# Graph attention on one core: a third tile picked in every fifth step, the edge bias written by ScalarE, picking from step 0 to 96, and one tile of sixteen steps fetched row by row from ScalarE's queue

## The chip, the core and the metric

The kernel runs on one core of a Trainium2 chip. The metric is the time of one execution on the device in microseconds (us). The kernel before takes 1790.06 us (median of three runs, 1789.95 to 1790.13). A profile is a trace of one further execution.

## The reference

One layer of graph attention with a residual and a layer norm. There are N = 6250 nodes with 64 features and E = 206250 edges, sorted by destination; four heads of 16.

```python
Qh = (x @ Wq.T + bq).reshape(n, H, D)
Kh = (x @ Wk.T + bk).reshape(n, H, D)
Vh = (x @ Wv.T + bv).reshape(n, H, D)
Ee = (edge_attr @ We.T + be).reshape(-1, H, D)
score = (Kh[src] * Qh[dst] * (1.0 / np.sqrt(D)) * Ee).sum(-1)
score = jnp.exp(jnp.clip(score, -5.0, 5.0))
msg = Vh[src] * score[..., None]
wV = jax.ops.segment_sum(msg, dst, num_segments=n)
x = _layernorm(x + wV.reshape(n, H * D))
```

## The kernel before

Edges are cut into 1612 tiles of 128, eight tiles to a group (202 groups). The main loop has 105 steps: 97 of two groups (16 tiles) and then 8 of one group.

A prologue computes a table of keys and values for every node (`kv_tab`, in DRAM) and a table of queries (`q3_tab`). The keys and values of the first four groups are computed directly from gathered rows of x (`xs`): a transpose, a copy by ScalarE and matmuls with `wkv`, half a group at a time.

In a step, the rows of `kv_tab` of each tile's 128 source nodes have to come into one of five buffers `kvs`. They get there in four ways:

- One indirect DMA for each tile, issued by POOL (`gather_kv`, L402). In step s the gathers of step s + 4 are issued; a buffer is free once the message of the step that used it is made.
- Two tiles of a step are **picked** by TensorE, two steps ahead of use, in steps 4 to 94. ScalarE writes the source numbers less 50 times the column (`sources`, L466), TensorE turns them into `from_b` (`sources_turned`, L471), VectorE compares them with block numbers (`hots`, L481, in two halves) and TensorE multiplies the one-hot matrix with the table of x in three bf16 parts (`picks`, L491, 25 matmuls a half). The three parts are added (`picked`, L498), turned (`picked_turned`), and multiplied with the weights (`picked_kv`, L513 to L516), whose result ScalarE copies to `kvs`.
- Every sixth step one tile is fetched row by row by 128 plain DMAs from SP's queue, spread over the six steps before (`fetch_rows`, L540 and L544; the row numbers are loaded to registers).
- The first four groups, as said.

The table of parts is made in the loop's first steps: SP loads pieces of x, ScalarE and VectorE split them (`table_parts`).

The rest of a step: `spread` (L555) and ScalarE's Square and Relu (`onehot_rows`, L572, and `onehot_rows_rest`, L577) make the one-hot rows of the next step's destinations; `queries` (L595) multiplies them with a window of queries; `edges` (L388 the bias, L391 the values) makes edge values in PSUM; `products` (L602, L603), `scores` (L609 to L612, with ScalarE's Exp), `message` (L619, L622) and `minus` (L630, L632) give the message in three bf16 parts; `sums` (L638) multiplies it with one-hot edges (L585), and `add` (L652) adds the result to an accumulator. When a block of 128 nodes is complete it is closed (L668 to L678), and later normalised and stored.

The order of all instructions on each engine is that in which the code emits them: the schedule is written by hand. Each engine works through its own list in that order, and waits where data or a buffer is not ready. In PSUM, `small` is one tile that holds the turned sources, the scores and the sums; `pb` is a single buffer used by `spread` and by `picked_turned` and `picked_kv`.

Of the kernel before, what the change touches and what calls it, by code (L numbers as in the profile page):

```python
# [40 lines left out]
TB = 8  # L41
M0 = 4
# [21 lines left out]
LAST = NS - 8 - 3  # L64


def picks_in(s):
    return M0 <= s <= LAST

# [5 lines left out]
COLUMN = 2 * G - 3  # L75
# [27 lines left out]
def tile_gnn(ctx: ExitStack, tc: tile.TileContext, x, xT, wT, bias, beT, weT, eT, src, dst, dst_rows,  # L103
# [52 lines left out]
    bkv_p = consts.tile([3, G // 2, 2 * C], BF16, name="bkv_p")  # L156
    minus_b = consts.tile([P, P], BF16, name="minus_b")
# [26 lines left out]
    with tc.tile_pool(name="nodes", bufs=1) as nodes, \  # L184
# [36 lines left out]
        nc.sync.dma_start(be_sb, beT.to_broadcast([3, C]))  # L221
        nc.vector.memset(we_sb, 0.0)
# [147 lines left out]
        for g in range(XG):  # L370
            for h in range(2):
                tp = npsum.tile([P, 2, P], F32, name="tp", bufs=2)
                for u in range(2):
                    j = 4 * h + 2 * u
                    nc.tensor.transpose(tp[:, u, :],
                                        XS[g][:, j:j + 2, :].rearrange("p j c -> p (j c)"), ident)
                xe = nodes.tile([P, 2, P], F32, name="xe", bufs=2)
                nc.scalar.activation(xe, tp, AF.Copy)
                pv = npsum.tile([P, 4, 2 * C], F32, name="pv", bufs=2)
                nc.tensor.matmul(pv, ones_b, bkv_p, start=True, stop=False, skip_group_check=True)  # L380
                for u in range(2):
                    nc.tensor.matmul(pv[:, 2 * u:2 * u + 2, :], xe[:, u, :], wkv, start=False,
                                     stop=u == 1, skip_group_check=True)
                nc.scalar.activation(kv_of(g)[:, 4 * h:4 * h + 4, :], pv, AF.Copy)

    def edge_values(pe, et, n):

        nc.tensor.matmul(pe[:, :n, :], ones_b, be_p[:, :n, :], start=True, stop=False,  # L388
                         skip_group_check=True)
        for u in range(n // 2):  # L390
            nc.tensor.matmul(pe[:, 2 * u:2 * u + 2, :], et[:, u, :], we_sb, start=False,  # L391
                             stop=u == n // 2 - 1, skip_group_check=True)
# [13 lines left out]
    for g in range(XG, 2 * KVB - 2):  # L406
        for j in range(G):
            gather_kv(g, j)
# [3 lines left out]
    with tc.If(rv == 0) as branch:  # L412

        with tc.tile_pool(name="work", bufs=2) as work, \
# [5 lines left out]
            col, from0, from1 = (small[:, i * C:(i + 1) * C].bitcast(BF16) for i in range(3))  # L420
            from_b = from0, from1
            score_all = small[:, 3 * C:3 * C + 2 * G * H]
            pa = small[:, 4 * C:7 * C].rearrange("p (i c) -> p i c", i=3)
            nc.tensor.transpose(col, row_b[:, 0:1].to_broadcast([P, P]), ident_b)

            parts = accp.tile([P, NB, 3, C], BF16, name="parts")
            nc.vector.memset(parts, 0.0)
            NX = N // NB
            x_v = x.rearrange("(p b) c -> p b c", p=NX)
            n_picks = LAST - M0 + 1  # L430
            src_f = accp.tile([P, n_picks, 2], F32, name="src_f")
            t0 = (M0 + 3) * 2 * G - 2
            for i in range(2):
                nc.vector.tensor_copy(src_f[:, :, i],
                                      src_i[:, t0 + i:t0 + i + 2 * G * (n_picks - 1) + 1:2 * G])
            pick = fixed.tile([P, 4 * P], F32, name="pick")
            rows3 = pick[:, :6 * C].rearrange("p (k i c) -> p k i c", k=2, i=3)
            HOT, FAR, X = {}, {}, {}
# [5 lines left out]
            def table_parts(b):  # L444

                n = min(TB, NB - b)
                raw = work.tile([P, TB, C], F32, name="raw", bufs=1)
                nc.sync.dma_start(raw[:NX, :n], x_v[:, b:b + n, :])
                rest = pick[:NX, :n * C].rearrange("p (b c) -> p b c", b=n)
                nc.scalar.activation(rest, raw[:NX, :n], AF.Copy)  # L450
                nc.scalar.activation(parts[:NX, b:b + n, 0], raw[:NX, :n], AF.Copy)
                return rest

            def table_parts_rest(b, rest):
                n = min(TB, NB - b)
                nc.vector.tensor_sub(rest, rest, parts[:NX, b:b + n, 0])
                nc.scalar.activation(parts[:NX, b:b + n, 1], rest, AF.Copy)
                nc.vector.tensor_sub(parts[:NX, b:b + n, 2], rest, parts[:NX, b:b + n, 1])

            def sources(s, i):  # L460

                if picks_in(s):
                    FAR[s, i] = work.tile([P, P], BF16, name="far")
                    nc.scalar.activation(FAR[s, i], row50, AF.Identity,  # L466
                                         bias=src_f[:, s - M0, i:i + 1], scale=-1.0)

            def sources_turned(s, i):
                if picks_in(s):  # L470
                    nc.tensor.transpose(from_b[i], FAR.pop((s, i)), ident_b)  # L471
# [4 lines left out]
            def hots(s, i, h):  # L476

                if picks_in(s):
                    HOT[s, i, h] = work.tile([P, NB // 2, P], BF16, name="hot", bufs=4)
# [6 lines left out]
            def picks(s, i, h):  # L486
                if picks_in(s):
                    hot = HOT.pop((s, i, h))
                    for k in range(NB // 2):
                        b = h * NB // 2 + k  # L490
                        nc.tensor.matmul(rows3[:, i], hot[:, k, :], parts[:, b], start=b == 0,  # L491
                                         stop=b == NB - 1)

            def picked(s):

                if picks_in(s):
                    xp = work.tile([P, 2, C], F32, name="xp")
                    nc.vector.tensor_reduce(xp, rows3.rearrange("p k i c -> p k c i"), axis=AX.X,  # L498
                                            op=OP.add)
                    X[s] = xp  # L500

            def picked_turned(s):
                if picks_in(s):
                    room = psum.tile([P, G, P], F32, name="pb")
                    nc.tensor.transpose(room[:, 0, :], X[s].rearrange("p k c -> p (k c)"), ident)
                    xe = work.tile([P, P], F32, name="xe")
                    nc.scalar.activation(xe, room[:, 0, :], AF.Copy)
                    X[s] = xe, room[:, 4:6, :]

            def picked_kv(s):  # L510
                if picks_in(s):
                    xe, kv = X.pop(s)
                    nc.tensor.matmul(kv, ones_b, bkv_p[:, :2], start=True, stop=False,  # L513
                                     skip_group_check=True)
                    nc.tensor.matmul(kv, xe, wkv, start=False, stop=True, skip_group_check=True)  # L515
                    nc.scalar.activation(kvs[(s + 2) % KVB][:, 2 * G - 2:, :], kv, AF.Copy)  # L516

            def gather(s):
                for g in groups_of(s):
                    for j in range(tiles_of(g)):  # L520
                        if is_rowed(s) and (g - STEPS[s][0]) * G + j == COLUMN:
                            continue
                        if not picks_in(s - 2) or g == STEPS[s][0] or j < G - 2:
# [21 lines left out]

            def rows_fetched(s):
                if is_rowed(s):
                    nc.scalar.activation(kvs[s % KVB][:, COLUMN, :], RK.pop(s), AF.Copy)

# [10 lines left out]
            def edges(s, k):  # L560

                g = STEPS[s][0] + k
                if k == 0:
                    PE[s] = psum.tile([P, 2 * G, C], F32, name="pe")
                edge_values(PE[s][:, k * G:(k + 1) * G], ET[g], tiles_of(g))
# [134 lines left out]
            closed, scaled, normed = 0, 0, 0  # L700
            keys(0)
# [5 lines left out]
            onehot_edges(0)  # L707
            for s in range(NS):
# [9 lines left out]
                if more:  # L718
                    onehot_rows(nexts[0], spread(nexts[0]))
                    onehot_rows_rest(nexts[0])  # L720
# [4 lines left out]
                if nexts[1:]:  # L725
                    onehot_rows(nexts[1], spread(nexts[1]))
                making = [b for b in range(s * 2 * TB, (s + 1) * 2 * TB, TB) if b < NB]
                if making:
                    rest = table_parts(making[0])
                prod = products(s)  # L730
                picked(s - 1)
                if more:
                    edges(s + 1, 0)
                picks(s, 0, 0)
                score = scores(s, prod)
                if nexts[1:]:
                    onehot_rows_rest(nexts[1])
# [5 lines left out]
                picked_turned(s - 1)  # L743
                if nexts[1:]:
                    edges(s + 1, 1)
                minus(s, msg, 0)
                hots(s, 1, 0)
                picks(s, 0, 1)
                minus(s, msg, 1)
                picked_kv(s - 1)  # L750
# [5 lines left out]
                picks(s, 1, 0)  # L756
                sources(s + 1, 1)
                sources(s + 2, 0)
                if s + 1 < NS:
                    rows_fetched(s + 1)  # L760
                if more:
# [5 lines left out]
                hots(s + 1, 0, 0)  # L767
                hots(s + 1, 0, 1)
# [14 lines left out]
                for i, b in enumerate(making):  # L783
                    if i:
                        rest = table_parts(b)
                    table_parts_rest(b, rest)
# [4 lines left out]
            scales(B - 2, B - 1)  # L791
            norm(B - 2)
# [170 lines left out]
```

## Time and profile before

| what | value |
|---|---|
| median of three runs | 1790.06 us |
| profiled execution | 1789.88 us |
| its span, first to last instruction | 1788.0 us |
| matmul busy | 1638.5 us, 15751 instructions |
| VectorE busy | 1481.6 us |
| ScalarE busy | 914.0 us |
| POOL busy | 1337.4 us |
| mean granted TensorE clock | 0.951 |

The span is what the trace covers; the execution's own time is 1.9 us longer. PE is TensorE's matmuls, PEld its weight loads, DVE VectorE, ACT ScalarE, POOL GpSimd, SP SyncE; a q after the name is an engine's own queue of DMA and semaphore instructions. A line of the groups gives source line, engine, operation, what is written from what, shapes and count, then busy time, mean length in ns, and the idle time ahead of it with what ended it. A line of the timeline gives start and length in us. In a line of the waits stand the total, the number and the longest.

### The profile page before, as it was taken

How to read it: one execution, taken by the hardware profiler on the slowest of the kernel's cores; microseconds unless marked ns; L12 is line 12 of the kernel's file. 1: busy time of each engine (PE TensorE's matmuls, PEld its weight loads, DVE VectorE, ACT ScalarE, POOL GpSimd, SP SyncE). 2: the span in 40 equal slices, each digit the busy share in tenths (PEclk: the TensorE clock that was granted, in tenths of full speed). 3: DMA queues.
4: the chain of work that ended last, by engine and by line, in shares of the span. 5: the costliest groups of instructions: out<-in, count | busy, mean ns of one | idle time of the engine just before them, and what ended most of it. 6: DMA issues, size and time to landing. Idle time of an engine off the chain costs nothing.

```text
span 1788.0 us, 44286 instructions
## 1 busy us (share of the span) xinstructions
PE 1638.5 (92%) x15751; PEld 1369.6 (77%) x15751; DVE 1481.6 (83%) x1695; ACT 914.0 (51%) x1328; POOL 1337.4 (75%) x1427
## 2 busy tenths in 40 slices
PE   8978999999999998999999899999989998999864
PEld 8647888888888787787887778777877887787632
DVE  6459999999998898888889888888988888898654
ACT  3465555555554464454455445455544554455443
POOL 7777777777777777777777777777777777777774
PEclk9968999999999999999999999999999999999855
DMA  7443333333333333332333333323332333333331
GB/s 221 132 121 84 90 93 94 93 94 92 93 81 94 93 86 89 92 94 80 93 93 81 93 81 93 92 81 99 87 93 80 94 93 81 93 90 81 91 80 44
DMA packets 109970, 166.71 MB, mean 93 GB/s; under 512 B 69196, under 2 KB 71452, under 8 KB 109626
## 3 DMA queue, kind: packets, MB, share of 16 engines
q0 software_dynamic: 45280, 91.78, 19.4%
q1 hardware_dynamic: 64074, 71.01, 14.1%
q8 instruction: 125, 2.05, 0.5%
q10 hardware_dynamic: 384, 1.00, 0.3%
q14 instruction: 107, 0.88, 0.2%
HBM read 156.33 MB, written 7.33 MB: 92 GB/s over the span
## 4 chain that ended last, share of the span: by engine, by line
PE 38%; POOL 29%; issue 14%; DVE 13%; DMA 4%; ACT 3%; DVEq 0%; SPq 0%; POOLq 0%; ACTq 0%
POOL kv L402 29%; PE pick L491 18%; PE pe L391 5%; DVE hot L481 5%; DMA kv<-kv_tab,src_i 3%; PE pq L630 2%; PE small L638 2%; DVE prod L603 2%; DVE prod L602 2%; PE pb L555 2%; PE pe L388 2%; PE pb L515 1%; PE pq L595 1%; DVE pq L619 1%; PE ps L350 1%
## 5 line engine op out<-in xcount | busy, mean ns | idle before, releaser
L402 POOL DMA_INDIRECT kv<-kv_tab,src_i x1383 | 1305.3, 944 | 421.7 <-issue 399.8
L491 PE MATMUL pick<-parts,hot 128*128 128x192 bf16 x9100 | 828.3, 249 | 0.0
L491 PEld LDWEIGHTS <-hot 128*128 128x128 bf16 x9100 | 771.7, 99 | 38.1
L481 DVE TENSOR_TENSOR hot<-small,block 128x3200 bf16<-128x3200 bf16 x364 | 645.3, 1813 | 0.4 <-PE pick L491 0.4
L572 ACT ACTIVATE to<-pb,minus_row 126x1024 bf16<-126x1024 f32 x202 | 222.7, 1102 | 371.0 <-PE pb L555 367.2
L632 ACT ACTIVATE msg<-pq 128x1024 bf16<-128x1024 f32 (+2 forms) x210 | 207.6, 989 | 222.3 <-PE pq L630 222.3
L391 PEld LDWEIGHTS pe<-we_sb,et 128*128 128x128 f32 x1612 | 209.7, 203 | 133.4 <-issue 95.3
L602 DVE TENSOR_TENSOR prod<-kv,pq 128x1024 f32<-128x1024 f32 (+2 forms) x105 | 123.5, 1176 | 169.3 <-DMA kv<-kv_tab,src_i 52.0
L391 PE MATMUL pe<-we_sb,et 128*128 128x128 f32 x1612 | 250.3, 302 | 0.0
L577 ACT ACTIVATE to<-to,one_p 126x1024 bf16<-126x1024 bf16 x202 | 230.6, 1142 | 3.5
L638 PEld LDWEIGHTS <-of 128*128 128x128 bf16 x1612 | 145.3, 102 | 31.1 <-issue 7.9
L638 PE MATMUL small<-msg,of 128*128 128x192 bf16 x1612 | 161.9, 257 | 0.5 <-ACT msg L632 0.5
L388 PE MATMUL pe<-be_p,ones_b 3*128 3x512 bf16 x202 | 79.7, 395 | 86.3 <-DVE prod L603 86.1
L630 PE MATMUL pq<-msg,minus_b 128*128 128x512 bf16 x404 | 128.0, 396 | 33.1 <-ACT msg L622 19.5
L622 ACT ACTIVATE msg<-pq 128x1024 bf16<-128x1024 f32 (+2 forms) x105 | 103.8, 989 | 96.8 <-DVE pq L619 96.8
L609 DVE TENSOR_REDUCE small<-prod 128x64 f32<-128x1024 f32 (+2 forms) x105 | 123.6, 1177 | 14.5 <-PE small L471 8.8
L555 PE MATMUL pb<-key_rows,ident_b 112*128 112x512 bf16 x403 | 127.9, 400 | 2.8 <-ACT to L572 2.8
L603 DVE TENSOR_TENSOR prod<-prod,pe 128x1024 f32<-128x1024 f32 (+2 forms) x105 | 123.6, 1177 | 3.6
L619 DVE TENSOR_TENSOR pq<-kv,small 128x1024 f32<-128x1024 f32 (+2 forms) x105 | 123.4, 1175 | 1.4 <-ACT small L612 1.4
L585 DVE TENSOR_TENSOR of<-small,key 128x2048 bf16<-128x2048 bf16 (+2 forms) x105 | 122.9, 1171 | 0.3
L595 PEld LDWEIGHTS <-to 126*128 126x128 bf16 x1612 | 63.5, 101 | 25.3 <-issue 25.1
L612 ACT ACTIVATE small<-small 128x64 f32<-128x64 f32 (+2 forms) x105 | 21.7, 207 | 111.1 <-DVE small L611 109.2
(129 smaller groups left out, 996.4 us busy)
## 6 DMA issues: line engine op xcount, KB each, us to landing
et<-in_eT SPq DMA_DIRECT2D x100, 512.0 KB
rk<-kv_tab SPq DMA_DIRECT2D x1920, 0.5 KB
kv<-kv_tab,src_i POOLq DMA_INDIRECT x1383
qw<-q_tab SPq DMA_DIRECT2D x202, 15.8 KB
kv_tab<-kv_sb SPq DMA_DIRECT2D x5, 640.0 KB
q_tab<-q SPq DMA_DIRECT2D x5, 480.0 KB
acc<-in_x SPq DMA_DIRECT2D x48, 32.0 KB
out<-y SPq DMA_DIRECT2D x48, 32.0 KB
```

Source lines behind the costliest of these rows:

```text
L391: nc.tensor.matmul(pe[:, 2 * u:2 * u + 2, :], et[:, u, :], we_sb, start=False, stop=u == n // 2 - 1, skip_group_check=True)
L402: nc.gpsimd.indirect_dma_start(out=kv_of(g)[:, j, :], out_offset=None, in_=kv_tab[:, :], in_offset=bass.IndirectOffsetOnAxis(ap=src_i[:, t ...
L481: nc.vector.tensor_tensor(HOT[s, i, h].rearrange("p b (a c) -> p b a c", c=2), pairs(from_b[i])[:, None].to_broadcast(shape), block2[:, bl ...
L491: nc.tensor.matmul(rows3[:, i], hot[:, k, :], parts[:, b], start=b == 0, stop=b == NB - 1)
L555: nc.tensor.matmul(pb[:, b:b + 4, :], ident_b[:NR2, g // 2:g // 2 + 1].to_broadcast([NR2, P]), key_rows[:, g % 2, b * P:(b + 4) * P], star ...
L572: nc.scalar.activation(TO[g][:, :n, :], pb[:3 * W, :n, :], AF.Square, bias=minus_row3[:3 * W])
L577: nc.scalar.activation(TO[g][:, :n, :], TO[g][:, :n, :], AF.Relu, bias=one_p[:3 * W], scale=-1.0)
L602: nc.vector.tensor_mul(prod[:, :n, :], kvs[s % KVB][:, :n, :C], PQ[s][:, :n, :])
L603: nc.vector.tensor_mul(prod[:, :n, :], prod[:, :n, :], PE[s][:, :n, :])
L630: nc.tensor.matmul(msg[:, lo:hi, :], minus_b, M3[s][:, lo:hi, i, :], start=False, stop=True, skip_group_check=True)
L632: nc.scalar.activation(M3[s][:, :n, i + 1, :], msg[:, :n, :], AF.Copy)
L638: nc.tensor.matmul(PA[s], OH[s][:, j, :], M3[s][:, j], start=j == 0, stop=j == n - 1)
```

## The change

Five edits, in one diff:

- **A third tile.** In every fifth step (0, 5 ... 90) a third tile is picked, with its own hots, picks into a `pb` tile (`R3`), reduction (`picked_third`), a 64-column turn and a share in `picked_kv`.
- **Picking from step 0 to 96.** The table of parts is no longer made in the loop but in the prologue, from `xT_sb` by 50 transposes, interleaved with the first groups' keys and values, whose next half is turned one half ahead. The first hots stand ahead of step 0.
- **ScalarE's bias.** The bias matmul of `edges` is gone except for step 0; ScalarE writes the bias to PSUM (`biases`) and the edge matmuls add to it. The tile is now a fixed one, `pe_all`.
- **Rows from ScalarE's queue.** One tile in each of the steps 20, 36, 52, 68 and 84 is fetched by 128 row DMAs from ScalarE's queue, eight in each of the sixteen steps before (`fetch_rows2`).
- **The order of a step.** `spread` of the first next group comes after `sources_turned` and not first; `edges` of both groups come after the message; `picked_turned` and `picked_kv` come later. At the end `scales` and `norm` of one block move behind `roots` of the last.

```diff
+LAST = NS - 8 - 1
+def is_rowed2(s):
+    return s % ROWED2 == OFF and ROWED2 < s < NS - 8
 def picks_in(s):
-    return M0 <= s <= LAST
+    return 0 <= s <= LAST
+def picks_third(s):
+    return picks_in(s) and s % THIRD == 0 and STEPS[s + 2][1] == 2
...
+        def parts_of_x(b):
+            n = min(TB, NB - b)
+            px = npsum.tile([P, 2, 2 * C], F32, name="ps").rearrange("p i (j c) -> p (i j) c", j=2)
+            px = px[:, :n]
+            for u in range(n):
+                nc.tensor.transpose(px[:, u, :], xT_sb[:C, (b + u) * P:(b + u + 1) * P],
+                                    ident[:C, :C])
+            nc.scalar.activation(parts[:, b:b + n, 0], px, AF.Copy)
+            nc.vector.tensor_sub(px, px, parts[:, b:b + n, 0])
+            halves.append((px, b, n))
+
+        def rest_of_x():
+            px, b, n = halves.pop(0)
+            nc.scalar.activation(parts[:, b:b + n, 1], px, AF.Copy)
+            nc.vector.tensor_sub(parts[:, b:b + n, 2], px, parts[:, b:b + n, 1])
+
+        order = [(g, h) for g in range(XG) for h in range(2)]
+        blocks = list(range(0, NB, TB))
+        xe = x_turned(*order[0])
+        for i, gh in enumerate(order):
+            following = x_turned(*order[i + 1]) if i + 1 < len(order) else None
+            for b in blocks[2 * i:2 * i + 2]:
+                parts_of_x(b)
+            first_kv(*gh, xe)
+            xe = following
+            while halves:
+                rest_of_x()
...
-        nc.tensor.matmul(pe[:, :n, :], ones_b, be_p[:, :n, :], start=True, stop=False,
-                         skip_group_check=True)
+        if not biased:
+            nc.tensor.matmul(pe[:, :n, :], ones_b, be_p[:, :n, :], start=True, stop=False,
+                             skip_group_check=True)
...
+            def picked_third(s):
+                if picks_third(s):
+                    to = R3.pop(s).rearrange("p g e -> p (g e)")[:, :3 * C]
+                    nc.vector.tensor_reduce(X[s][:, 0], to.rearrange("p (i c) -> p c i", i=3),
+                                            axis=AX.X, op=OP.add)
...
+            def fetch_rows2(s):
...
+                if k == 0:
+                    RS[to, 2] = work.tile([1, P], I32, name="rs2")
+                    t = STEPS[to][0] * G + COLUMN2
+                    nc.sync.dma_start(RS[to, 2], src_rows[t:t + 1, :])
+                    RK[to, 2] = work.tile([P, 2 * C], F32, name="rk2")
+                lo = k * ROWS
+                _, vs = nc.values_load_multi_w_load_instructions(
+                    RS[to, 2][:, lo:lo + ROWS], engines=[mybir.EngineType.Activation], min_val=0,
+                    max_val=N, skip_runtime_bounds_check_because="sources are nodes")
+                for i, v in enumerate(vs):
+                    nc.scalar.dma_start(RK[to, 2][lo + i:lo + i + 1, :], kv_tab[bass.ds(v, 1), :])
...
+            def biases(s):
+                n = tiles_in(s)
+                nc.scalar.activation(pe_all[:, :n, :], be_all[:, None, :].to_broadcast([P, n, C]),
+                                     AF.Copy)
...
             for s in range(NS):
...
-                if more:
-                    onehot_rows(nexts[0], spread(nexts[0]))
-                    onehot_rows_rest(nexts[0])
                 if s:
                     sums(s - 1)
                 sources_turned(s, 1)
                 sources_turned(s + 1, 0)
-                if nexts[1:]:
-                    onehot_rows(nexts[1], spread(nexts[1]))
...
+                sources_turned(s, 2)
                 prod = products(s)
                 picked(s - 1)
+                picked_third(s - 1)
                 if more:
-                    edges(s + 1, 0)
+                    onehot_rows(nexts[0], spread(nexts[0]))
                 picks(s, 0, 0)
                 score = scores(s, prod)
-                if nexts[1:]:
-                    onehot_rows_rest(nexts[1])
+                if more:
+                    biases(s + 1)
+                    onehot_rows_rest(nexts[0])
...
-                picked_turned(s - 1)
                 if nexts[1:]:
-                    edges(s + 1, 1)
+                    onehot_rows(nexts[1], spread(nexts[1]))
+                for k in range(len(nexts)):
+                    edges(s + 1, k)
                 minus(s, msg, 0)
+                if nexts[1:]:
+                    onehot_rows_rest(nexts[1])
                 hots(s, 1, 0)
                 picks(s, 0, 1)
+                picked_turned(s - 1)
                 minus(s, msg, 1)
-                picked_kv(s - 1)
...
                 hots(s, 1, 1)
                 picks(s, 1, 0)
+                picked_kv(s - 1)
                 sources(s + 1, 1)
                 sources(s + 2, 0)
+                sources(s + 1, 2)
...
+                fetch_rows2(s)
...
                 picks(s, 1, 1)
-                hots(s + 1, 0, 0)
-                hots(s + 1, 0, 1)
+                for h in range(2):
+                    hots(s, 2, h)
+                for h in range(2):
+                    picks(s, 2, h)
+                for h in range(2):
+                    hots(s + 1, 0, h)
```

## The prediction

> **What bounds the kernel now.** I read the page's busy shares first, then the list of waits, the groups, the windows, and last the timeline of a few stretches.
>
> ```profile
> span 1788.0 us, 44286 instructions
> PE 1638.5 (92%) x15751; PEld 1369.6 (77%) x15751; DVE 1481.6 (83%) x1695; ACT 914.0 (51%) x1328; POOL 1337.4 (75%) x1427
> ```
>
> By busy share TensorE looks like the bound. The waits and groups say otherwise:
>
> ```profile
> POOL kv L402 <- issue: 399.8, 1311, 0.3
> DVE prod L602 <- DMA kv<-kv_tab,src_i: 52.0, 34, 4.0
> ...
> L402 POOL DMA_INDIRECT kv<-kv_tab,src_i x1383 | 1305.3, 944 | 421.7 <-issue 399.8
> L491 PE MATMUL pick<-parts,hot 128*128 128x192 bf16 x9100 | 828.3, 249 | 0.0
> L481 DVE TENSOR_TENSOR hot<-small,block 128x3200 bf16<-128x3200 bf16 x364 | 645.3, 1813 | 0.4 <-PE pick L491 0.4
> L388 PE MATMUL pe<-be_p,ones_b 3*128 3x512 bf16 x202 | 79.7, 395 | 86.3 <-DVE prod L603 86.1
> ```
>
> POOL's 75% is 0.944 us per gather with 0.30 us between two of them, never more: (1305.3 + 421.7) / 1383 = 1.249 us apiece. The first of the 32 xs gathers starts at 2.80; 1415 gathers later the last starts at 1768.85. POOL never stops.
>
> ```profile
> 1768.85 0.94 POOL L402 DMA_INDIRECT kv<-kv_tab,src_i  x1 [0.30 <-issue]
> ...
> 796.16 0.94 POOL L402 DMA_INDIRECT kv<-kv_tab,src_i  x1 [0.30 <-issue]
> ...
> 799.11 1.22 DVE L602 TENSOR_TENSOR prod<-kv,pq 128x1024 f32<-128x1024 f32 x1 [3.05 <-DMA kv<-kv_tab,src_i]
> ```
>
> The gather at 796.16 is step 44's last (counting 14 per step, 13 in a rowed one); its product starts 2.0 us after that gather ends. But it was not always so. With the count laid along the timeline, step 5's gathers end 38 us before its product, step 15's 21 us, step 25's 6.5, and from step 28 on about 2. The windows show the two stages:
>
> ```profile
> 208.40:396.70 188.30, 188.30 (x1971) 161.24 (x1969) 176.98 (x183) 103.28 (x146) 142.26 (x152) 1.00 0.34 92
> ...
> 990.00:1697.00 707.00, 653.00 (x6615) 553.66 (x6613) 598.04 (x628) 356.60 (x498) 534.43 (x567) 0.98 0.33 89
> ```
>
> The columns are length, PE, PEld, DVE, ACT, POOL. Until step 28 TensorE is busy without a gap and a step lasts 188.30 / 12 = 15.69 us; afterwards POOL sets 17.2. So POOL is the bound of the whole, with TensorE only 1.5 us a step behind it, and VectorE (176.98 / 12 = 14.75) just behind that. What POOL gives back is worth only as much as these two allow.
>
> **POOL's part.** After the change: 1612 tiles, less 32 (xs), 2 x 97 picked, 19 thirds (steps 0, 5 ... 90), 15 rowed and 5 newly rowed = 1347 gathers, 36 fewer: 36 x 1.249 = 45 us. Its step falls to 17.0.
>
> **A later start.** The table of parts moves into the prologue: 50 small transposes. Their nearest row is this, 216 ns each:
>
> ```profile
> 33.58 18.15 PE L350 MATMUL ps<-w_sb,xT_sb 65*128 65x64 f32 x84 [0.68 <-DVE q L341]
> ...
> 59.09 2.08 PE L382 MATMUL pv<-wkv,xe 128*128 128x256 f32 x4
> ...
> 328.99 0.70 PE L515 MATMUL pb<-wkv,xe 128*128 128x256 f32 x2
> ```
>
> 10.8 us, less 1.4 that turning the next half early saves, plus 0.4 for the first far tile ahead of step 0: about 10 us. ScalarE's 26 copies (0.38 each, as L322 of that shape) and VectorE's 26 subtractions of the same size lie beside TensorE's 34 us; VectorE's 4.06 us memset of the table goes, and the 3.54 of hots ahead of step 0 takes its place while ScalarE makes the one-hot rows. Here a rule must be weighed. The prologue's fp32 matmuls go at half the loop's speed (four in 2.08 against two in 0.70), and the 84 above stay slow through 18 us without a pause. The Trainium skill, "TensorE: Matmul & The Clock Gate", part 1, has the array warm after about 3.4 us of sustained work; then a denser prologue would run warm, and the table would cost 5 us or nothing. By the row it costs 10. I take the row, and keep 2 to 12. So step 0's product moves from 84.97 to 95.
>
> POOL feels that: step 5's gathers reuse step 0's buffer and need its message (L619), which ended 6.6 us after its product, so about 101.7. POOL would be there at 43.0 + 41 x 1.249 = 94.2, and loses 7.5; step 0, now with a third, is longer than 17.5 and costs it one more. Later it has room. POOL alone then gives 1788 - 45 + 9 = 1752.
>
> **TensorE's step.** Start to start in the step at 318.48: picks 4 x 2.06, sums 1.32, edges 2 x 1.0, bias matmuls 2 x 0.31, the rest 3.46, in all 15.64. The bias matmuls go: 15.02. A third adds two picks (4.12) and about 0.5 of transposes and key-value work, in one step of five: 15.95 on average. A 2 us wait would make the first picks of a step slow (3.6 us for 25 at 821, against 2.23), so waits are not free.
>
> **VectorE's step.** It is 14.47 (302.52 to 316.99) without closing a block, some 1.2 more with, every second step. It includes a wait that stays, score and sums being in one PSUM tile:
>
> ```profile
> 307.14 0.42 DVE L652 SCALAR_TENSOR_TENSOR acc<-small,above,acc 128x192 f32<-128x192 f32 x1 [0.28 <-ACT small L612]
> ...
> 308.93 3.54 DVE L481 TENSOR_TENSOR hot<-small,block 128x3200 bf16<-128x3200 bf16 x2
> ```
>
> A third adds 3.54 of hots and 0.35 of reduction (as the last row of its kind, L696): 0.8 on average, 15.9. Two engines at 15.9 disturb each other. Walking ten steps by these durations, in the new order: plain steps 14.5 and 16.2 in turn, a third step 18 to 19.5, the step after it 14.8 to 16.8 (TensorE is 2 us late there, spread waits for picked_third to give back pb, and the score for sources_turned). Five steps: 81.1 and 79.9, so 16.1. The norms (32 in the loop x 0.25), two root batches of 4 us and 7 keys of 0.65 add 0.2: 16.3.
>
> **ScalarE.** The biases (104 x 1.02, as L622 of that shape) lie in its idle time (103.28 of 188.30 busy), but behind Exp; edges moved behind them meet TensorE just as it is done with picks and spread. With that cover gone each 1 us late would be 1 us of TensorE. Rows: 80 steps issue 8 each, after a register load. SP has the price, loads included:
>
> ```profile
> 306.11 11.82 SPq L544 DMA_DIRECT2D rk<-kv_tab  x24
> ```
>
> 0.49 each, 3.9 us on ScalarE's sequencer per step. The cover is ScalarE's wait for the next spread (3.99 us before L572 at 303.38; ACT to L572 <- PE pb L555 is 367 us in all). Queued behind the issues are Square, then Exp, and VectorE's add and message wait for Exp. I find the gap 3 to 4 us and take 0.1 a step. In five steps ScalarE also waits about 2 us for the index row, whose DMA stands behind SP's 24 row issues. Bounds: 0, and 1 us in 80 steps. The rows themselves land steps before they are read, on DMA engines that are a third busy. SP loses 7 table loads and gains 6 small ones; it has room. The reordered end swaps three small operations: nothing.
>
> **Sum.** 16.4 a step: 95 + 97 x 16.4 = 1686 for step 97's product, then the eight short steps and the end. That part is 79.1 now at POOL's pace (1708.9 to 1788.0); a short step's own chain is 8.6 to 9.2 (the two between 1728.8 and 1746.7), so 75; plus 1 for a cold step 0. Span 1762, against 1752 from POOL alone: VectorE and TensorE, not POOL, would hold the last word. The profiled execution took 1789.88, 1.9 over its span, and the median is 0.2 above it: 1764.
>
> **Rivals.** *POOL stays the bound to the end* (0.22). If a step is under 16.2, computing catches POOL before the end: 1752 + 2 = 1754, or 1747 with a warm prologue. For it: both engines' sums are under 16. Against: they have no slack between them, and POOL's lead starts at some 50 us and shrinks by 0.6 a step. *VectorE and TensorE pace it* (0.57): 1764, and up to 16.6 a step makes 1783, and POOL's floor of 1754 is the other end. *Slower: ScalarE's row issues delay Exp* (0.17). From 16.66 a step (1788 - 95 - 76 over 97) nothing is gained; that is 0.27 above my figure, or 0.33 us more delay in each of 80 steps. At 1.0 us more it is 1764 + 80 = 1844. For it: the gap is no longer than the issues. Against: two or three xT issues on ScalarE's queue at the start cost 0.61 each and the same on SP 0.68, so ScalarE isn't the slower issuer. The last 0.04 is a tie at 1790.
>
> **Numbers.** A change of 0.2% (3.6 us) is about the least that a measurement of this kernel can tell from none. Faster 0.77, same 0.04, slower 0.19 (a few of the second case's misses join the third). The range, 1747 to 1798, leaves out the larger part of the slow case and a little below.
>
> **What would show it.** Right: 1347 gathers; POOL, for the first time, waiting for VectorE (L602 or L619's successors) in the first steps and again through most of the loop; product to product 16.4 on average, 18 to 19.5 in every fifth; no waits for kv DMAs before about step 80; no pause on ScalarE's row issues that Exp waits for. Wrong: gathers back to back to the end (then 1754), steps above 16.7 with VectorE waiting on Exp (then slower), or step 0's product at 86 (the prologue was cheaper).

## The result, and the profile after

The changed kernel takes 1864.29 us (median of four runs, 1852.87 to 1865.06) against 1790.01 for the kernel before on the same chip: a ratio of 1.040, 95% interval 1.0366 to 1.0434. The forecast was 1764, with a range to 1798. The change costs 74 us where 26 were to be gained. The profiled execution took 1865.05 us, its span is 1863.0.

The page's first lines and its costliest group, the gathers:

```profile
span 1863.0 us, 49671 instructions
PE 1690.0 (91%) x17263; PEld 1481.1 (80%) x17263; DVE 1595.5 (86%) x1796; ACT 1009.1 (54%) x1504; POOL 1303.5 (70%) x1391
...
L456 POOL DMA_INDIRECT kv<-kv_tab,src_i x1347 | 1271.4, 944 | 502.7 <-issue 388.0
```

The 1347 gathers are there. Their idle time is 502.7 us, of which only 388.0 is issue: POOL stands still for 115 us for other reasons, where it was 22 before. The list of waits says for what (columns: engine and line, what it waited for, us in all, times, longest):

```profile
POOL kv L456 <- issue: 388.0, 1272, 0.3
...
ACT to L664 <- DMA rk<-kv_tab: 110.8, 17, 23.1
POOL kv L456 <- DVE pq L711: 89.3, 17, 15.0
...
PE pb L642 <- ACT to L664: 41.4, 8, 18.8
...
PE pe L445 <- DMA et<-in_eT: 25.7, 9, 3.4
```

Read from below: TensorE waits for edge values (et) that SP should have loaded long before, and for ScalarE's Square (L664), up to 18.8 us at a time. POOL waits for a buffer, that is for the message (L711). The head of it is ScalarE, whose Square stood behind row transfers (rk) for 110.8 us, once for 23.1. And SP's own queue has a wait that the kernel before didn't have:

```profile
SPq L612 <- DMA rk<-kv_tab: 191.9, 80, 8.8
...
SPq L202 <- DMA rk<-kv_tab: 27.1, 8, 4.4
...
SPq L188 <- DMA rk<-kv_tab: 11.5, 4, 4.1
```

L612 are SP's row issues, L202 and L188 its loads of the query windows and of the edge values. The transfers that they wait for are ScalarE's rows (L629): the row buffers of the two queues have the same name.

The time from one step's product to the next shows where it goes. In most stretches of five steps it is 16.1 to 17 us on average, about as forecast, and four times there is a jump:

| steps | five steps before the jump | the jump |
|---|---|---|
| 15 to 19 | 80.6 (10 to 14) | 106.3, of which step 19 is 37.0 |
| 30 to 34 | 81.4 (25 to 29) | 107.1, of which step 34 is 37.8 |
| 50 to 54 | 86.2 (45 to 49) | 97.8, steps 50 and 51 together 49.6 |
| 65 to 69 | 81.0 (60 to 64) | 106.0, of which step 67 is 35.0 |

The timeline around the second of the long pauses, first of ScalarE, then of SP (start, length, engine, line):

```profile
404.15 0.68 ACT L512 ACTIVATE far<-row,src_f 128x128 bf16<-128x128 f32 x2
424.42 3.45 ACTq L629 DMA_DIRECT2D rk<-kv_tab  x8
427.92 1.11 ACT L664 ACTIVATE to<-pb,minus_row 126x1024 bf16<-126x1024 f32 x1 [23.09 <-DMA rk<-kv_tab]
```

```profile
398.97 7.30 SPq L612 DMA_DIRECT2D rk<-kv_tab  x16
...
409.94 11.83 SPq L612 DMA_DIRECT2D rk<-kv_tab  x24
421.82 0.24 SPq L622 DMA_DIRECT2D rs<-in_src_rows  x1
```

ScalarE has nothing more to do at 404.83 and then waits for the row of indices (L622). SP issues that at 421.82, because it is a whole step behind: the 24 row issues of this step begin only at 409.94. The eight issues themselves take 3.45 us. The wait named in the third line, "DMA rk", is thus mostly a wait for the index row.

How far SP is ahead can be counted: from its first load of a query window for a step (L202) to that step's product it is 27.2 us in step 10, 23.6 in step 16, 11.7 in step 19; after the pause 35.6 in step 22, then 27.3, 25.4 and 17.9 in steps 25, 31 and 34, and another pause. SP loses some ten to twenty us of lead in sixteen steps and gets it back when everything else stands still. (In experiment 2, without ScalarE's rows, the four fives of the table take 82.8, 83.8, 81.7 and 84.1 us: the jumps are some 85 of the 104 us by which step 97's product is later here.)

### The profile page after: what moved, and what is told of

Read it like the earlier page. It is cut to its first block, busy times and chain, and to the rows that moved or that the text cites. A ratio compares the mean times of both kernels' runs of the same rounds, so it can differ in the third digit from the quotient of the medians.

```text
span 1863.0 us, 49671 instructions
## 1 busy us (share of the span) xinstructions
PE 1690.0 (91%) x17263; PEld 1481.1 (80%) x17263; DVE 1595.5 (86%) x1796; ACT 1009.1 (54%) x1504; POOL 1303.5 (70%) x1391
## 4 chain that ended last, share of the span: by engine, by line
PE 43%; DVE 16%; POOL 14%; issue 9%; DMA 7%; ACT 5%; SPq 4%; ACTq 2%; DVEq 0%; POOLq 0%
PE pick L542 19%; POOL kv L456 14%; DVE hot L528 7%; PE pe L445 7%; PE pq L722 3%; PE small L730 3%; SPq L612 2%; DMA et<-in_eT 2%; PE pb L642 2%; ACT to L664 2%; DVE prod L695 2%; DVE prod L694 2%; DMA kv<-kv_tab,src_i 2%; PE pb L578 2%; PE pb L542 1%
## 5 line engine op out<-in xcount | busy, mean ns | idle before, releaser
L456 POOL DMA_INDIRECT kv<-kv_tab,src_i x1347 | 1271.4, 944 | 502.7 <-issue 388.0
L542 PEld LDWEIGHTS <-hot 128*128 128x128 bf16 x10650 | 888.8, 98 | 123.7 <-issue 59.3
L542 PE MATMUL pick<-parts,hot 128*128 128x192 bf16 x9700 | 869.7, 247 | 46.5 <-DVE xp L556 46.2
L528 DVE TENSOR_TENSOR hot<-small,block 128x3200 bf16<-128x3200 bf16 x426 | 754.0, 1813 | 2.6 <-PE pick L542 1.8
L664 ACT ACTIVATE to<-pb,minus_row 126x1024 bf16<-126x1024 f32 x202 | 223.9, 1108 | 480.6 <-PE pb L642 344.2
L445 PE MATMUL pe<-we_sb,et 128*128 128x128 f32 x1612 | 227.4, 299 | 47.5 <-DMA et<-in_eT 25.7
L730 PE MATMUL small<-msg,of 128*128 128x192 bf16 x1612 | 155.0, 251 | 0.5 <-ACT msg L724 0.5
L583 ACT ACTIVATE kv<-pb 128x256 f32<-128x256 f32 (+1 forms) x97 | 39.2, 404 | 190.2 <-PE pb L578 133.4
L730 PEld LDWEIGHTS <-of 128*128 128x128 bf16 x1612 | 137.7, 100 | 1.9 <-issue 1.5
L711 DVE TENSOR_TENSOR pq<-kv,small 128x1024 f32<-128x1024 f32 (+2 forms) x105 | 123.4, 1175 | 0.3 <-ACT small L704 0.3
L744 DVE SCALAR_TENSOR_TENSOR acc<-small,above,acc 128x192 f32<-128x192 f32 x103 | 43.0, 417 | 82.5 <-ACT small L704 81.4
L656 ACT ACTIVATE pe<-be_all 128x1024 f32<-128x1024 f32 (+1 forms) x104 | 102.1, 982 | 0.0
```

Source lines behind the costliest of these rows:

```text
L456: nc.gpsimd.indirect_dma_start(out=kv_of(g)[:, j, :], out_offset=None, in_=kv_tab[:, :], in_offset=bass.IndirectOffsetOnAxis(ap=src_i[:, t ...
L528: nc.vector.tensor_tensor(HOT[s, i, h].rearrange("p b (a c) -> p b a c", c=2), pairs(from_b[i])[:, None].to_broadcast(shape), block2[:, bl ...
L542: nc.tensor.matmul(to, hot[:, k, :], parts[:, b], start=b == 0, stop=b == NB - 1)
L664: nc.scalar.activation(TO[g][:, :n, :], pb[:3 * W, :n, :], AF.Square, bias=minus_row3[:3 * W])
L730: nc.tensor.matmul(PA[s], OH[s][:, j, :], M3[s][:, j], start=j == 0, stop=j == n - 1)
```

## The experiments

| kernel | us | ratio to before, 95% |
|---|---|---|
| changed | 1864.29 | 1.0366 to 1.0434 |
| 1: index row earlier | 1850.41 | 1.0330 to 1.0374 |
| 2: without ScalarE's rows | 1757.55 | 0.9800 to 0.9833 |
| 3: index earlier, no third tile | 1811.40 | 1.0110 to 1.0144 |
| 4: kernel before, with ScalarE's rows | 1850.78 | 1.0323 to 1.0358 |
| 5: index earlier, no rows on SP | 1802.58 | 1.0051 to 1.0085 |
| 6: one issue a step on ScalarE | 1775.53 | 0.9875 to 0.9941 |
| 7: all rows by SP | 1756.22 | 0.9798 to 0.9830 |
| 8: no ScalarE rows, third tile in one step of four | 1774.98 | 0.9891 to 0.9927 |
| 9: no ScalarE rows, ScalarE held | 1761.09 | 0.9808 to 0.9841 |
| 10: index earlier, fewer rows on SP | 1794.09 | 0.9998 to 1.0020 |
| 11: no ScalarE rows, no third tile | 1781.60 | 0.9921 to 0.9954 |
| 12: one issue on ScalarE, no rows on SP | 1775.06 | 0.9879 to 0.9912 |

The kernel before took 1789.82 beside the first four experiments, 1790.01 beside the next four and 1792.68 beside the last four; a difference between one of the last four and another kernel is uncertain by these 3 us.

**1. The index row, two steps earlier.**

```diff
+            def fetch_index2(s):
+                to = s + 4 + ROWED2
+                if is_rowed2(to):
+                    RS[to, 2] = work.tile([1, P], I32, name="rs2")
+                    t = STEPS[to][0] * G + COLUMN2
+                    nc.sync.dma_start(RS[to, 2], src_rows[t:t + 1, :])
...
+                fetch_index2(s)
                 fetch_rows(s)
```

> The changed kernel with one move: the 128 row numbers that ScalarE loads to registers are fetched by SP two steps before ScalarE first needs them, not in the same step behind SP's own row issues. Theory (a wait for the row numbers holds ScalarE, and everything behind it, in steps 2, 18, 34, 50 and 66): the idle times of 16 to 23 us before L664 go, steps stay at 16.4, and the time falls from 1864 to 1773 +- 8. Rival 1 (the eight row issues in each of 80 steps are what costs): 1855 or more. Rival 2 (VectorE and TensorE have too much work with the third tile): 1855 or more, with even steps of 17.5.

Measured: 1850.41, only 13.9 better, and the runs of the two kernels overlap (1842.77 to 1857.94 here, 1852.87 to 1865.06 there). The long pauses are gone, but the steps from 15 on are longer throughout: 17.8 us on average in steps 18 to 81, against 18.1 in the changed kernel, pauses included. The index row was where the loss was paid, not what it came from. SP's queue, then the engines' waits:

```profile
SPq L612 <- DMA rk<-kv_tab: 191.6, 83, 7.4
...
SPq L202 <- DMA rk<-kv_tab: 50.7, 15, 7.0
```

```profile
ACT to L668 <- DMA rk<-kv_tab: 110.4, 29, 6.0
...
PE pe L445 <- DMA et<-in_eT: 72.2, 27, 5.4
POOL kv L456 <- DVE pq L715: 64.9, 18, 7.1
```

SP waits as long as before for ScalarE's rows, in short pieces, and TensorE's wait for edge values has gone from 25.7 to 72.2 us. SP's lead now stays at 11 to 23 us.

**2. Without ScalarE's rows**, their five tiles gathered by POOL.

```diff
 def is_rowed2(s):
-    return s % ROWED2 == OFF and ROWED2 < s < NS - 8
+    return False
```

> The changed kernel without row fetching on ScalarE's queue: the five tiles go back to POOL (1352 gathers). Theory: no wait either, so 1770 to 1782, within 6 us of the kernel with early row numbers; five gathers more are 6 us at most, and only if POOL sets the end. Rival 1 (the issues in 80 steps cost): at least 20 us below the kernel with early row numbers.

Measured: 1757.55. So this one edit costs 1864.29 - 1757.55 = 107 us, and all others together gain 32. From the page:

```profile
span 1758.4 us, 47673 instructions
PE 1669.0 (95%) x17263; PEld 1462.3 (83%) x17263; DVE 1593.3 (91%) x1796; ACT 1006.3 (57%) x1499; POOL 1308.5 (74%) x1396
...
L456 POOL DMA_INDIRECT kv<-kv_tab,src_i x1352 | 1276.4, 944 | 416.6 <-issue 391.2
```

The 17263 matmuls are the same and VectorE has the same work; POOL waits for next to nothing. The step is 16.39 us on average from step 0 to 96, and SP's lead stays at 28 to 36 us in steps 15 to 81.

**3. Index row earlier, no third tile.** Does the third tile make ScalarE or TensorE too late for its rows?

```diff
 def picks_third(s):
-    return picks_in(s) and s % THIRD == 0 and STEPS[s + 2][1] == 2
+    return False
...
```

> Early row numbers, and no third tile: 19 more gathers, 38 fewer hots, 950 fewer picks. Theory: a step of TensorE and VectorE is then 15.4 to 15.6, POOL's 17.2, so POOL sets the end: 1752 + 24 + 2 = 1778, within 10 us of the kernel with early row numbers. Rival 2 (too much work with the third tile): 50 us or more below it.

Measured: 1811.40. The same waits are there (SP's row issues for ScalarE's rows 186.9 us), so the third tile is not their cause; but the loss is smaller. Experiment 11 gives the base without ScalarE's rows: 1781.60. The rows cost 30 us here and 93 with the third tile (1850.41 - 1757.55). But the difference does not lie in the steps in which ScalarE issues rows: the table under experiment 4 has them.

**4. The kernel before, with ScalarE's rows alone** (its index row late, as in the changed kernel): `ROWED2`, `COLUMN2`, `fetch_rows2` and its part in `rows_fetched` and `gather` are put in, and nothing else.

> The kernel before with one part of the change: five tiles fetched by rows from ScalarE's queue, with the row numbers fetched late as in the changed kernel. Theory: ScalarE stands as long, about 15 us in four steps, but here POOL sets 17.2 a step and the rest needs 15.7, so the delay is made up in some ten steps while POOL goes on: 1790 - 6 = 1784, at most 1794. Rival 3 (a stand of ScalarE costs its length wherever it falls): 1784 + 60 = 1844.

Measured: 1850.78, 61 us slower than before, where a slight gain had been expected. The cause needs none of the other edits. SP's row issues wait for ScalarE's rows 155.3 us in 68 waits.

The profiles of these kernels, from product to product in us a step. ScalarE issues rows in steps 2 to 81:

| kernel | steps 2 to 81 | steps 82 to 96 |
|---|---|---|
| before | 16.73 | 16.88 |
| 4: before, with ScalarE's rows | 17.83 | 15.33 |
| changed | 17.79 | 15.90 |
| 1: index row earlier | 17.53 | 15.91 |
| 2: without ScalarE's rows | 16.42 | 16.27 |
| 3: index earlier, no third tile | 17.33 | 15.26 |
| 11: no ScalarE rows, no third tile | 16.63 | 17.03 |

While both queues fetch rows a step takes 17.3 to 17.8 us in all four kernels, with a third tile or without, and 16.4 to 16.7 in the three without ScalarE's rows. The losses in the whole time differ mostly by what follows. After step 81 the kernels with rows are faster than their bases (before for 4, experiment 11 for 3, experiment 2 for the other two), most of all where POOL sets the base's pace: in steps 82 to 96 the product waits 13.6 us for gathers in experiment 11 and 1.4 in experiment 3, where POOL seems to have got ahead meanwhile. So of 0.70 x 80 = 56 us lost, experiment 3 wins 27 back; experiment 4 wins 23 of 88 back, experiment 1 only 5 of 89. A common pace is what one would see if a loop through both queues set the step; that loop's length has not been worked out.

**5. Index row earlier, no rows on SP** (15 tiles more for POOL).

```diff
 def is_rowed(s):
-    return s % ROWED == 0 and 2 * ROWED <= s < NS - 8
+    return False
```

> The changed kernel with the index row fetched two steps earlier, and SyncE's own row fetches switched off: their 15 tiles go back to POOL, ScalarE's five tiles stay by rows. Theory C (SyncE and ScalarE wait for each other's row transfers, so that a loop SyncE's issues, landing, ScalarE's issues, landing becomes longer than the step; SyncE's own work is 13.3 us a step, 10.5 of it rows): with SyncE's rows gone the loop is short, and POOL decides: against the kernel without ScalarE's rows (1757.6) ten gathers more of 1.25 us, 1770; range 1765 to 1785. Rival I (the eight issues of 3.5 to 4 us a step on ScalarE hold up its next activations by themselves): no better than with SyncE's rows, 1835 to 1855.

Measured: 1802.58, between the two theories. 48 of the 93 us are gone with SP's rows, but not all. ScalarE still waits:

```profile
ACT to L668 <- DMA rk<-kv_tab: 148.9, 29, 8.3
```

A wait of this line includes the issues themselves. By the trace's records of the single DMAs, ScalarE's row issues themselves wait 52.6 us for SP's loads of edge values and 18.5 for SP's loads of x for closed blocks. SP now waits for TensorE or VectorE before many of these loads, since it is early, and a load that it has only just issued is one that ScalarE then waits for.

**6. One issue a step on ScalarE.** One transfer of eight rows takes the place of the register load and the eight issues. Its rows come from a fixed place in the table, so the kernel leaves out fetching these five tiles' own rows. (The index row is fetched earlier here too, and no longer used.)

```diff
-                _, vs = nc.values_load_multi_w_load_instructions(
-                    RS[to, 2][:, lo:lo + ROWS], engines=[mybir.EngineType.Activation], min_val=0,
-                    max_val=N, skip_runtime_bounds_check_because="sources are nodes")
-                for i, v in enumerate(vs):
-                    nc.scalar.dma_start(RK[to, 2][lo + i:lo + i + 1, :], kv_tab[bass.ds(v, 1), :])
+                nc.scalar.dma_start(RK[to, 2][lo:lo + ROWS, :], kv_tab[lo:lo + ROWS, :])
```

> The changed kernel, with ScalarE's register load and eight row issues of each step put into one transfer of eight rows from a fixed place (so those five tiles get rows that are not the edges'); SyncE's rows stay. Theory C: one ScalarE transfer in each step is enough to tie the two queues: SyncE's 13.3 us, some 2 us to land, ScalarE's one issue and 2 us to land make about 17.5 us a step in place of 16.4, 1800 to 1850. Rival I (the length of ScalarE's issues): 3.5 to 4 us a step become 0.5, and it is 1752 to 1762.

Measured: 1775.53, 18 us above the kernel without ScalarE's rows: neither theory's number. SP's queue, then TensorE's wait for edge values:

```profile
SPq L612 <- DMA rk<-kv_tab: 180.9, 56, 6.9
```

```profile
PE pe L445 <- DMA et<-in_eT: 30.4, 22, 4.4
```

SP's row issues wait nearly as long for ScalarE as in experiment 1, and SP's lead is as short (10.5 to 23 us). But ScalarE doesn't wait for rows any more, and TensorE's wait for edge values is 30.4 us and not 72.2. So where SP waits for ScalarE but ScalarE not for SP, 18 of the 93 us are left.

**7. All rows by SP**, and SP's first row tile in one step of eight in place of six, so that SP issues 24 rows a step (and the index row earlier, as in experiment 1).

```diff
-ROWED = 6
+ROWED = 8
...
-                    RS[to, 2][:, lo:lo + ROWS], engines=[mybir.EngineType.Activation], min_val=0,
+                    RS[to, 2][:, lo:lo + ROWS], engines=[mybir.EngineType.SP], min_val=0,
...
-                    nc.scalar.dma_start(RK[to, 2][lo + i:lo + i + 1, :], kv_tab[bass.ds(v, 1), :])
+                    nc.sync.dma_start(RK[to, 2][lo + i:lo + i + 1, :], kv_tab[bass.ds(v, 1), :])
```

> The changed kernel with the index row earlier, the five tiles' rows issued by SyncE in place of ScalarE, and SyncE's other row tile in one step of eight in place of six, so that SyncE issues 24 rows a step as its fullest steps do now, 15 us of issue at 0.42 us each with its other work. Theory C: one queue has no other to wait for; 16 tiles by rows against 15 in the kernel without ScalarE's rows: 1757, range 1750 to 1765. Rival L (more rows of 512 B at a time, whoever issues them, crowd out the loads and gathers): 1800 or more.

Measured: 1756.22, with 16 tiles by rows. The rows are no burden for the memory or the DMA engines; that they come from a second queue is. With the kernel of experiment 2 this is the fastest measured, 1.9% faster than before (interval of the ratio 0.9798 to 0.9830); the two can't be told apart.

**8. No ScalarE rows, the third tile in one step of four** (`THIRD = 4`).

> The kernel without ScalarE's rows (1757.6), with the third tile in one step of four in place of five: some four gathers fewer (5 us of POOL), four times 4.6 us more of TensorE. If POOL decides there, 1752; if TensorE's pace does, 1770 to 1778. The two were worked out to be within some us of each other, so 1755 to 1775.

Measured: 1774.98. Five gathers fewer and 17 us more: the step is 16.55 us. More picking is past the point where TensorE and VectorE take over from POOL.

**9. No ScalarE rows, but ScalarE held** for as long as the issues took.

```diff
+            def held(s):
+                if 2 <= s < 82:
+                    idle = work.tile([P, HELD], BF16, name="idle", bufs=1)
+                    nc.scalar.activation(idle, parts.rearrange("p b i c -> p (b i c)")[:, :HELD], AF.Copy)
...
-                fetch_rows2(s)
+                held(s)
```

> The kernel without ScalarE's rows (1757.6) plus one activation of 3584 elements of no use in steps 2 to 81, where ScalarE's register load and row issues stood: it holds ScalarE for some 3.7 us, the time of eight row issues, and sends no transfer. Theory C2 (what costs is that the two queues wait for each other; ScalarE stands there idle some 4 us a step waiting for PE's pb anyway): 1755 to 1775. Rival I (ScalarE held so long before its Square is enough): 1800 or more, since the kernel with the issues but without SyncE's rows took 1802.6.

From the groups, the operation that was added:

```profile
L635 ACT ACTIVATE idle<-parts 128x3584 bf16<-128x3584 bf16 x80 | 254.2, 3177 | 0.0
```

Measured: 1761.09. 80 times 3.18 us of ScalarE, at the place of the issues, are 254 us, and the time is 3.5 us above experiment 2, uncertain by 3. Eight issues take as long as this activation: 3.17 us in the median of the changed kernel's 80. So their length is hidden, as the prediction had it (its 0.1 a step is 8 us).

**10. Index row earlier, fewer rows on SP** (`ROWED = 8`: 16 rows a step, where it was 16 or 24).

> The changed kernel with the index row earlier (1850.4), and SyncE's row tile in one step of eight in place of six: 16 rows a step in place of 16 or 24, so SyncE's own work is some 2.2 us a step less. If a loop through both queues sets the step (17.9 us a step on average in steps 2 to 81, against 16.4), it gets 2.2 us shorter and falls under 16.4: 1765 to 1790, with 5 us of POOL for four gathers more. If the cost belongs to ScalarE's issues whatever SyncE does: 1835 to 1850.

Measured: 1794.09, above the expected 1765 to 1790, but 56 better than experiment 1. (In the trace of experiment 1 a step of 2 to 81 takes 17.5 us, not the 17.9 of the expectation; here it is 17.0.) What is left is no longer on SP's side, whose lead is 30 to 40 us:

```profile
ACT to L668 <- DMA rk<-kv_tab: 210.3, 42, 8.6
```

In the stretch from 400 to 1200 us SP's row issues wait 21.2 us in all, where they waited 117.3 in experiment 1. But ScalarE's row issues wait for SP's loads, as in experiment 5: 45.3 us for edge values and 14.7 for loads of x. SP with slack waits for TensorE before such a load, and hands this on to ScalarE. So ScalarE's wait for SP has a price of its own, too: the kernel is 36.5 us above experiment 2 (uncertain by 3), with one gather less.

**11. No ScalarE rows, no third tile.**

> The kernel without ScalarE's rows (1757.6) and without the third tile: 19 gathers more on POOL, 23.7 us at 1.25 us each, and 4.6 us less of TensorE in each of 19 steps. If POOL is then the bound: 1775 to 1782. If POOL was not at its bound at 1757.6: less than 1770.

Measured: 1781.60, 24.0 us above experiment 2 (uncertain by 3); 19 gathers of 1.25 us are 23.7. Without the third tile POOL is the bound. With it in one step of five it still nearly is, and in one step of four (experiment 8) no longer: from the start of the last gather to the end of the span it is 22.5 us here, 23.6 in experiment 2 and 46.3 in experiment 8.

**12. One issue a step on ScalarE, no rows on SP.** As in experiment 6, the five tiles get other rows than their own.

> One transfer of eight rows a step on ScalarE from a fixed place (those tiles get rows that are not the edges'), and SyncE's rows off, their 15 tiles with POOL: the base for the kernel with ScalarE's eight issues and no rows on SyncE (1802.6). POOL's bound with ten gathers more than the kernel without ScalarE's rows: 1770, range 1765 to 1778. If the ties between the queues alone, not the eight issues, make the 1802.6: 1795 or more.

Measured: 1775.06. It is the base of experiment 5: with SP's rows gone, eight issues cost 27.5 us more than one (1802.58 - 1775.06). Holding ScalarE has no such price (experiment 9), so these are, as far as shown, the waits for SP's transfers.

**What ties the queues.** The trace's records of the plain DMAs show on which semaphore each waits before it starts, and which it raises when it has landed. The main loop's plain DMAs of SP and of ScalarE raise eight between them (100, 102 to 107, 109), and nearly every one waits first for what the last DMA on the same semaphore has raised, whichever queue that was in. From the changed kernel (start in us, queue, line, semaphore waited for and raised):

```
204.63 SP  L612 105
207.66 ACT L629 102
208.28 ACT L629 104
208.67 ACT L629 106
...
210.09 SP  L612 106   waited 5.05 us, for the row that ACT issued at 208.67
210.50 SP  L612 107
```

SP has nothing to do with ScalarE's row, but its next issue is next on semaphore 106, and so it waits until ScalarE has got so far in its own list (207.66) and the row has landed. In the other direction, in experiment 10, ScalarE's row at 411.72 waits 1.85 us on semaphore 104, for SP's load of edge values that SP issued at 408.20. Eight issues in a row raise four to eight different semaphores (most often six in the changed kernel, all eight in 14 of 80 steps of experiment 10), so they have to wait for most of SP's last transfers, often the newest too. A single issue waits for one: in experiment 6 it had been issued at least 5.7 us before, and ScalarE's list of waits has none for it.

## Why the prediction was wrong

**The step that failed** is the paragraph on ScalarE: "In five steps ScalarE also waits about 2 us for the index row ... Bounds: 0, and 1 us in 80 steps", which entered the sum with "I find the gap 3 to 4 us and take 0.1 a step", and, of SP, "it has room". The rows cost 107 us, 1.3 us in each of 80 steps. Three things in it were seen and priced rightly or nearly: the length of eight issues (3.9 us forecast; 3.17 us in the median of 80, 3.45 on average, 6.4 the longest), the gap that covers them (experiment 9), and that the index row stands behind SP's row issues. What was not asked was what SP's queue and ScalarE's have in common. The two queues were treated as independent, so SP's 24 issues could only be late for the index row, by 2 us. In the runs SP's issues wait for ScalarE's rows, lose lead at every step, and the index row is then 17 us late. The upper bound was a bound on the delay of ScalarE alone, and so the range was too narrow as well.

**The slow rival had the right number and another mechanism.** "At 1.0 us more it is 1764 + 80 = 1844" was close, but by row issues that delay Exp by their length. By experiment 9 they don't.

**The rest held in its sum.** Experiment 2 is the forecast without the rows: 0.1 x 80 = 8 us less than 1764, 1756; measured 1757.55. That it agrees so well is in part luck: the start was forecast 3.4 us too late, 97 steps of 16.3 are 9 us too short, and the median lies 2.7 us below the execution that was profiled.

- *The step*: 16.3 without rows; 16.39 measured, with 17 to 20 us in every fifth.
- *The later start*: step 0's product at 95; it stands at 91.6 in the changed kernel. The transposes were taken at 216 ns from a row of fp32 matmuls. They took less, eight in 1.11 us, 139 ns each: 6.9 us for 50 and not 10.8.

```profile
32.96 18.16 PE L371 MATMUL ps<-w_sb,xT_sb 65*128 65x64 f32 x84 [0.70 <-DVE q L362]
52.21 1.11 PE L416 MATMUL ps<-ident,xT_sb 64*128 64x64 f32 x8
53.79 2.08 PE L405 MATMUL pv<-wkv,xe 128*128 128x256 f32 x4
```

- *The clock*: the 84 matmuls take 18.16 us (18.15 before) and the four of `pv` 2.08, so a denser prologue didn't run at the loop's speed. In that the row was right against the rule of the Trainium skill, "TensorE: Matmul & The Clock Gate", part 1, by which the start would have been at 86. The granted clock itself is not on record there: the trace's first record of it stands at 93.0 us. The prediction's "half the loop's speed" is not what its rows say: four in 2.08 and two in 0.70 are 0.52 and 0.35 us each, two thirds of the speed, and since the ends of matmuls are modelled the factor is uncertain.
- *POOL*: forecast to wait for VectorE through most of the loop. Without ScalarE's rows it doesn't: after 116 us its gathers run back to back to the last at 1734.8. That is the prediction's own sign for the first rival, "POOL stays the bound to the end". Its 1754, with five gathers more, is 1760, and the profiled execution took 1760.27. So the case that was given 0.57 is not what experiment 2 shows, though the two forecasts lie too close to be told apart by the time alone; experiment 8 shows how near the other engines are.
- *The end*: from step 97's product 75 us forecast, 1758.4 - 1681.6 = 76.8 in experiment 2.

**What stays open.** How the 1.1 us that a step loses in experiment 1 divide among single waits has not been worked out, nor whether a loop through both queues, of a length that could be computed beforehand, sets the 17.3 to 17.8 us. Rows on ScalarE with semaphores of their own were not tried; they would be the direct test.

## What to carry to other kernels

A second DMA queue is not independent of the first because its engine is: look in the trace which semaphores the DMAs of both wait for. If they share a few in turn, each queue can be held by the other's last transfers, and an engine that computes hands its delays to a queue that was to run ahead. Many small transfers in a row were the worse case here, since they take most of the semaphores: one larger transfer in their place cost 18 us and not 93, and the same small ones on the queue that already had such rows (and fewer of its own) cost nothing that could be measured. And a stall at one load says only where a lost lead is paid: measure the lead of the queue over the loop before moving the load.

## What the runs showed of the hardware that was not expected

- As this program is built, plain DMAs of two queues waited for each other through eight shared semaphores: SP's row issues 191.9 us for ScalarE's rows, though they share neither buffer nor data.
- Eight row issues from ScalarE's queue took 3.17 us in the median of 80, as long as an activation of 3.18 us at the same place, whose 80 instances moved the time by 3.5 us, uncertain by 3.
- An fp32 transpose of 64 columns took 139 ns where an fp32 matmul of 64 columns took 216 ns, both in the prologue.
